# Graph attention and eight experts on one core: column tiles taken by twos, with more buffers for their weights

## Chip, core and metric

The kernel runs on one core of a Trainium2 chip. The metric is the device time in microseconds (us) of one launch. The kernel before takes 1325.94 us, the median of three runs (1325.19 to 1327.08). The profiled execution, from which the views below are taken, spans 1330.1 us from its first instruction to its last, at a mean granted TensorE clock of 0.991.

## What is computed

One layer: graph attention over 4096 nodes with 256 features and four heads, then a mixture of eight experts of which each node takes two. Cut to what matters here:

```python
h = einsum('nd,hdk->hnk', layernorm(x), W)           # 4 heads of 64
e = leaky_relu(s_row[:, :, None] + s_col[:, None, :], 0.2)
e = where(adj[None] > 0, e, NEG_INF)
att = softmax(e, axis=-1)
h_prime = einsum('hij,hjk->hik', att, h)
y = elu(h_prime) + x @ Wr + br                       # heads side by side
x = x + gamma * layernorm(y) + beta
x = x + moe(layernorm(x))                            # top 2 of 8, gelu(x @ W1) @ W2
```

The change is in the softmax's weights and in the two sums over them: the numerator (weights times h) and the denominator (weights summed).

## The kernel before

Output rows are taken in four stages of R = 1024 (the loop over a, line 1218); call them stage 0 to stage 3. Within a stage the loop over j (line 1220) takes 32 column tiles of 128 nodes. For each column tile:

- `load_mask` (line 1087) fetches 128 x 1024 numbers of the adjacency (three buffers) and ScalarE makes a bf16 mask of them (L1092 and L1093, three buffers).
- `weigh` (line 1199) makes the weights on VectorE: for each of the four heads one instruction (L1205) writes `w`, 128 x 1024 in fp32, as the larger of the row factor `er` and the column factor `eb`, times the mask. Each `w` lies in one of ten buffers of a pool, so a column tile takes four buffers, and ten buffers are two and a half tiles.
- `attend` (line 760) sums on TensorE. `sum_rows` (line 741) multiplies each head's weights, in two halves of 512 rows, with `ha`, a 128 x 64 block; two heads lie side by side in the columns of the array, and the results gather in four PSUM banks `acc`. `sum_weights` (line 750) multiplies the same weights with `unit`, two columns wide; four heads lie side by side, and the denominators gather in `den`. Each is eight matmuls per tile, and each of these is two records in the trace (fp32). Below, R stands for the rows of one column tile (16 records on L745) and W for its weights (16 records on L754).

A weights buffer is free again when both sums of its tile have read it. `queue` (line 407) chains the matmuls of both sums in the order in which they are written, so TensorE takes them in exactly that order. `attend` writes R before W for even tiles and for the last, and W before R for the others: R0 W0 W1 R1 R2 W2 W3 R3 and so on. TensorE thus changes between the two forms once per tile.

Other work lies between. In stage 0, blocks of 512 nodes are normed (`norm_block`, line 567), turned and projected (`project_block`, line 593) as the tiles need them; the first four tiles are done in halves of 512 rows. In stages 1 to 3 `finish_blocks` (line 917) carries the stage before to its end in steps, one per column tile: transposes on TensorE (L931, L960), elu, the norm (VectorE's L972, L975, L983, L989), the experts' choice (`route_rows`, line 780). These instructions are not in the chain of `queue`; a scheduler places them when the program is built. In stage 3 the plan of the first experts' tiles and the load of `w10`, the first expert's weights, are placed before the end (`first_tile`, line 1076). `mean_of_h` (line 714) needs all blocks and follows stage 0. After stage 3 come the experts: no weights of the attention are made there.

## Time and profile before

| | |
|---|---|
| median of 3 runs | 1325.94 us |
| span of the profiled execution | 1330.1 us |
| first rows of stage 0, 1, 2, 3 | 36.4, 282.3, 463.5, 644.5 us |
| end of the attention on TensorE | 826.7 us |
| TensorE, VectorE, ScalarE busy | 1287.9, 868.8, 574.1 us |

The page gives, for each engine, its busy time and its share of the span; then the span in 40 equal slices, each digit the busy share in tenths; then the costliest groups of instructions, each with line, engine, output<-inputs, shapes, count, busy time and the mean of one in ns, and after the second bar the idle time of the engine just before them and what ended it. A busy time of TensorE is a union of pipelined matmuls whose ends are modelled. The timeline merges neighbouring instructions of one kind: start, length, engine, line, names, shapes, count. The view of waits gives for each pair who waited for whom: total, number of times, longest.

### The profile page before, as it was taken

What the parts mean: (1) busy time and instruction counts of PE and PEld (TensorE: products, weight loads), DVE (VectorE), ACT (ScalarE), POOL (GpSimd) and SP (SyncE); (2) the same over time, 40 slices, a digit from 0 to 9 for tenths busy, and PEclk for the clock granted to TensorE, in tenths of its full rate; (3) what the DMA queues carried; (4) which work ended last, traced back from release to release, by engine and by line L of the source; (5) the groups of instructions that cost most, each with busy time, mean ns of one, the idle gap of its engine ahead of it and who ended that gap; (6) DMA issues with size and microseconds to landing.
All of it is one profiled execution on the core that took longest, in us unless ns stands there. A gap on an engine that the chain in (4) does not pass through costs nothing.

```text
span 1330.1 us, 19232 instructions
## 1 busy us (share of the span) xinstructions
PE 1287.9 (97%) x7019; PEld 679.3 (51%) x7019; DVE 868.8 (65%) x1746; ACT 574.1 (43%) x1016; POOL 232.5 (17%) x190
## 2 busy tenths in 40 slices
PE   6899999999999999999999999999999999999997
PEld 4423344322232222232222323888888877888886
DVE  4899887789999989999899996655111111121110
ACT  3423333346764457644576432533333332323332
POOL 1000000000005300015000150125222222122222
PEclk9899999999999999999999999999899999999999
DMA  5525243343443535534333342987756786888772
GB/s 164 204 84 174 96 111 96 112 158 100 131 136 109 194 98 140 138 107 153 96 111 111 106 133 60 350 249 213 245 155 188 189 183 146 197 203 209 175 208 53
DMA packets 144145, 202.42 MB, mean 152 GB/s; under 512 B 49728, under 2 KB 113872, under 8 KB 143392
## 3 DMA queue, kind: packets, MB, share of 16 engines
q1 hardware_dynamic: 122448, 161.26, 40.7%
q0 software_dynamic: 19360, 32.53, 10.9%
q10 hardware_dynamic: 2224, 7.22, 1.4%
q8 instruction: 59, 0.97, 0.3%
q14 instruction: 54, 0.44, 0.1%
HBM read 171.89 MB, written 29.08 MB: 151 GB/s over the span
## 4 chain that ended last, share of the span: by engine, by line
PE 57%; DMA 19%; DVE 17%; issue 5%; ACT 1%; another core or an unknown queue 0%; POOLq 0%; ACTq 0%; DVEq 0%
PE acc L745 24%; DMA out<-o,ids 18%; PE den L754 12%; DVE w L1205 12%; PE po L1384 8%; PE ph L1355 7%; PE pr L629 1%; PE ph L605 1%; DMA xb<-in_x 1%; DVE y L983 1%; DVE y L975 1%; PE pt L584 1%; DVE y L972 1%; PE pt L1337 1%; DVE y L989 0%
## 5 line engine op out<-in xcount | busy, mean ns | idle before, releaser
L1205 DVE SCALAR_TENSOR_TENSOR w<-er,eb,am 128x1024 f32<-128x1024 f32 x496 | 610.0, 1286 | 44.5 <-PE den L754 41.3
L745 PE MATMUL acc<-w,ha 128*64 128x512 f32 x2048 | 466.2, 599 | 5.3 <-DVE w L1205 4.6
L745 PEld LDWEIGHTS acc<-w,ha 128*64 128x64 f32 x2048 | 137.7, 137 | 301.6 <-issue 281.0
L1359 ACT ACTIVATE hT<-ph,bias 128x256 f32<-128x256 f32 (+1 forms) x264 | 126.3, 480 | 296.5 <-PE ph L1355 205.2
L1092 ACT ACTIVATE am<-adj 128x1024 bf16<-128x1024 int32 x124 | 131.1, 1057 | 283.8 <-DVE w L1205 275.2
L1355 PE MATMUL ph<-xT,w 128*128 128x256 f32 (+1 forms) x1056 | 242.3, 387 | 4.0 <-ACT hT L1359 2.5
L754 PE MATMUL den<-w,unit 128*2 128x512 f32 x2048 | 238.2, 592 | 5.5 <-DVE w L1205 5.5
L1384 PE MATMUL po<-w,hT 128*128 128x256 f32 x1088 | 241.9, 381 | 0.0
L1384 PEld LDWEIGHTS po<-w,hT 128*128 128x128 f32 x1088 | 206.7, 191 | 28.2
L1355 PEld LDWEIGHTS ph<-xT,w 128*128 128x128 f32 x1056 | 200.5, 190 | 39.4 <-ACT hT L1359 3.1
L1393 DVE SCALAR_TENSOR_TENSOR o<-po,share,b2s 128x256 f32<-128x256 f32 x67 | 32.3, 483 | 268.3 <-PE po L1384 246.8
L1396 POOL DMA_INDIRECT out<-o,ids x67 | 104.9, 1566 | 345.0 <-DMA out<-o,ids 215.6
L754 PEld LDWEIGHTS den<-w,unit 128*2 128x2 f32 x2048 | 43.5, 84 | 174.5 <-issue 151.8
L1093 ACT ACTIVATE am<-am 128x1024 bf16<-128x1024 bf16 x124 | 130.9, 1057 | 3.0
L909 POOL DMA_INDIRECT lists<-xe,at x64 | 92.0, 1437 | 134.3 <-DVE missed L888 39.5
L993 POOL DMA_DIRECT2D out<-y x6 | 4.7, 782 | 329.3 <-issue 155.6
L1341 DVE COPY xT<-pt 128x256 f32<-128x256 f32 x13 | 5.5, 423 | 66.3 <-PE pt L1337 66.3
L605 PE MATMUL ph<-wall,xT 128*128 128x264 f32 x112 | 30.6, 393 | 0.3 <-DVE sc L615 0.3
L1376 ACT ACTIVATE b2s<-b2b,share 128x256 f32<-128x256 f32 x68 | 30.8, 503 | 0.0
L629 PE MATMUL pr<-wr,xT 128*128 128x256 f32 x112 | 29.0, 384 | 0.2 <-ACT xT L588 0.2
L187 ACT ACTIVATE m<-y,off 128x256 f32<-128x256 f32 x48 | 23.8, 497 | 10.5 <-DVE off L184 10.5
L962 ACT ACTIVATE y<-ptr,z 128x64 f32<-128x64 f32 x96 | 22.0, 313 | 8.7 <-PE ptr L960 8.7
(316 smaller groups left out, 655.8 us busy)
## 6 DMA issues: line engine op xcount, KB each, us to landing
w<-in_L_ffn_W SPq DMA_DIRECT2D x66, 1024.0 KB
adj<-in_adj SPq DMA_DIRECT2D x128, 512.0 KB
er<-parts ACTq DMA_DIRECT2D x3, 2048.0 KB
b2b<-in_L_ffn_b SPq DMA_DIRECT2D x33, 128.0 KB
early<-lists SPq DMA_DIRECT2D x16, 260.0 KB
residual<-rb POOLq DMA_DIRECT2D x8, 512.0 KB
rb<-residual SPq DMA_DIRECT2D x8, 512.0 KB
out<-y POOLq DMA_DIRECT2D x8, 512.0 KB
```

The source lines that it names most:

```text
L605: nc.tensor.matmul(ph, xT[:, c, ts(t, P)], wall[:, c, :], start=(c == 0), stop=(c == DC - 1),)
L629: nc.tensor.matmul(pr[:, t % 2, :], xT[:, c, ts(t, P)], wr[:, c, :], start=(c == 0), stop=(c == DC - 1),)
L745: queue(nc.tensor.matmul(acc[half][h // 2][ts(h % 2, K), :], ha[:, j, ts(h, K)], w[half][h], start=(j == 0), stop=(j == NT - 1),))
L754: queue(nc.tensor.matmul(den[h * Q : h * Q + HB, :], unit[:, j, h, 1 - half : 1 - half + HB], w[half][h], start=(j == 0 and half == 0), st ...
L909: ins = nc.gpsimd.indirect_dma_start(lists, bass.IndirectOffsetOnAxis(ap=at[:, k, t : t + 1], axis=0), xe[:, t, :], None,).ins
L1092: nc.scalar.activation(am, at[:, 0], AF.Relu)
L1093: nc.scalar.activation(am, am, AF.Sign)
L1205: nc.vector.scalar_tensor_tensor(wh[:, these], er[:, these, h], eb[:, j, h : h + 1], mask[:, these], op0=OP.max, op1=OP.mult,)
L1355: order_of(nc.tensor.matmul(ph, job["w1"][:, c, ts(f, P)], xT[:, c, :], start=(c == 0), stop=(c == DC - 1),))
L1359: job["gelu"] = nc.scalar.activation(hT[:, f, :], ph, AF.Gelu, bias=job["bias"][:, f : f + 1]).ins
L1384: order_of(nc.tensor.matmul(po, hT[:, f, ts(k, CH)], w2[:, f, :], start=(f == 0), stop=(f == FC - 1)))
L1396: nc.gpsimd.indirect_dma_start(job["into"], bass.IndirectOffsetOnAxis(ap=ids[:, k : k + 1], axis=0), o, None, compute_op=OP.add,)
```

## The change

`attend` now takes column tiles by twos. For the first two of a group of four it writes R0 R1 W0 W1, for the next two W2 W3 R2 R3, so that TensorE changes the form once per two tiles; the last two tiles of a stage take rows first again. The first tiles of stage 0, done in halves, keep the old order. A tile's weights are thereby held longer, and `kept` keeps the first tile of a pair until its second sum.

For that, buffers are added from memory that lies idle: two halves of `w10` (which isn't loaded before stage 3), and, from the end of stage 0, the two turned blocks `turned[0]` and `turned[1]`, which only stage 0 reads. So there are 12 buffers in stage 0, 14 in stages 1 and 2, and 12 in stage 3, where `w10` is needed for its load. `made_w` counts the weights made and deals them out in turn: first the spare ones, then the ten of the pool. The lengthening of the file moves later lines by 13 (up to `weigh`) and up to 26.

```diff
+        kept = []
+
         def attend(w, j, halves):
-            rows_first = j % 2 == 0 or j == NT - 1
-            for add in (sum_rows, sum_weights) if rows_first else (sum_weights, sum_rows):
-                add(w, j, halves)
+            if len(halves) < HB:
+                for add in (sum_rows, sum_weights) if j % 2 == 0 else (sum_weights, sum_rows):
+                    add(w, j, halves)
+                return
+            both = (sum_rows, sum_weights)
+            if j // 2 % 2 and j < NT - 2:
+                both = (sum_weights, sum_rows)
+            both[0](w, j, halves)
+            if j % 2 == 0:
+                kept.append(w)
+            else:
+                both[1](kept.pop(), j - 1, halves)
+                both[1](w, j, halves)
...
                     for h in range(H):
-                        wh = work.tile([P, HB, B], F32, tag="w", name="w", bufs=10)
+                        nth = made_w[0] % (10 + len(spare))
+                        made_w[0] += 1
+                        if nth < len(spare):
+                            wh = spare[nth]
+                        else:
+                            wh = work.tile([P, HB, B], F32, tag="w", name="w", bufs=10)
...
+                made_w = [0]
+                spare = [w10[:, c].rearrange("p (s r) -> p s r", s=HB) for c in range(DC)]
...
                     er = later
+                    if a == 0:
+                        spare += [turned[b].rearrange("p (s c) r -> p s (c r)", s=HB) for b in (0, 1)]
+                    if a + 2 == NR:
+                        del spare[:DC]
```

## The prediction

> **What bounds the kernel now.** I read the page first: busy shares, slices, costliest groups.

> ```profile
> PE 1287.9 (97%) x7019; PEld 679.3 (51%) x7019; DVE 868.8 (65%) x1746; ACT 574.1 (43%) x1016; POOL 232.5 (17%) x190
> PE   6899999999999999999999999999999999999997
> DVE  4899887789999989999899996655111111121110
> L1205 DVE SCALAR_TENSOR_TENSOR w<-er,eb,am 128x1024 f32<-128x1024 f32 x496 | 610.0, 1286 | 44.5 <-PE den L754 41.3
> L745 PE MATMUL acc<-w,ha 128*64 128x512 f32 x2048 | 466.2, 599 | 5.3 <-DVE w L1205 4.6
> L754 PE MATMUL den<-w,unit 128*2 128x512 f32 x2048 | 238.2, 592 | 5.5 <-DVE w L1205 5.5
> ```

> TensorE is full everywhere; VectorE is nearly full until the attention ends, at 826.7 us, and then nearly idle. So the change, all in the attention, works where two engines are both close to the limit. The windows of stages 1 to 3 (a = 1, 2, 3) put a number on that:

> ```profile
> 282.00:463.00 181.00, 178.78 (x1115) 50.52 (x1115) 171.65 (x231) 102.64 (x163) 34.45 (x20) 1.00 0.44 132
> 463.00:644.00 181.00, 179.09 (x1109) 50.52 (x1103) 170.93 (x227) 104.36 (x164) 26.76 (x20) 1.00 0.43 123
> 644.00:826.00 182.00, 178.92 (x1107) 51.50 (x1103) 168.22 (x251) 92.29 (x152) 25.17 (x18) 1.00 0.33 103
> ```

> Columns are width, then busy PE, PEld, DVE. VectorE has 9 to 14 us to spare in 181. The waits of stage 3 say who waits:

> ```profile
> DVE w L1205 <- PE den L754: 4.8, 5, 2.7
> PE den L754 <- DVE w L1205: 1.4, 2, 0.9
> ```

> VectorE waits for buffers more than TensorE for weights. Now the pitch, from TensorE's timeline in a quiet stretch of stage 2 (start, length, count):

> ```profile
> 598.59 7.09 PE L745 MATMUL acc<-w,ha 128*64 128x512 f32 x32
> 605.60 3.62 PE L754 MATMUL den<-w,unit 128*2 128x512 f32 x32
> 609.15 7.09 PE L745 MATMUL acc<-w,ha 128*64 128x512 f32 x32
> 616.17 3.62 PE L754 MATMUL den<-w,unit 128*2 128x512 f32 x32
> ```

> Two column tiles take 609.15 - 598.59 = 10.56 us. A block of 16 rows matmuls alone lasts 3.65, one of 32 7.09, so one tile's rows (R) cost 3.44; likewise weights (W) 3.62 - 1.90 = 1.72. Two of each are 10.32; the remaining 0.24 is two switches between R and W, 0.12 each. And VectorE beside it:

> ```profile
> 607.52 9.68 DVE L1205 SCALAR_TENSOR_TENSOR w<-er,eb,am 128x1024 f32<-128x1024 f32 x8 [0.88 <-PE den L754]
> 618.08 6.08 DVE L1205 SCALAR_TENSOR_TENSOR w<-er,eb,am 128x1024 f32<-128x1024 f32 x5 [0.88 <-PE den L754]
> ```

> Eight w in 9.68 with the last lasting 1.28: pitch 1.20, a tile 4.8 us. VectorE stands 0.88 us, then starts 607.52 - 605.60 = 1.92 us after the W that frees its buffer began. I use that: a buffer last read by a W is filled again from 1.92 us after that W's start.

> [...] 0.12 us at each change between the 64-column and the 32-column form, nothing between W and W. [...] The VectorE records of before stand in program order.

> **The change part by part.** *Switches.* In the order in which the two programs put the matmuls, changes of form (R, W, other) per stage go 75 to 75, 65 to 43, 62 to 45, 58 to 39. In stage 0 norms and projections fall between more blocks, so nothing is won. Stages 1 to 3 lose 22, 17 and 19, at 0.12: 2.6, 2.0 and 2.3 us, 7.0 in sum, on TensorE and so on the path, if weights are there in time.

> *The wait it adds.* Take four tiles in the new order, R0 from 0: R0 R1 to 6.88, W0 from 7.0, W1 8.72, W2 10.44, W3 due 12.16, R2 from 14.0, R3 to 20.88. That is 20.88 for 21.12 before. Each tile takes four buffers, and a W needs all four. With 12 buffers (stages 0 and 3) tile 3 reuses tile 0's, read last by W0: VectorE may start at 7.0 + 1.92 = 8.92 and ends at 8.92 + 3 x 1.20 + 1.28 = 13.8, when W3 was due at 12.16. TensorE stands 1.64 us in every four tiles: 22.52 for 21.12, 1.4 worse. Queued behind W3 are R2 and R3, nothing else can pass. With 14 buffers (stages 1, 2) only the last two w of tile 3 wait: 8.92 + 1.20 + 1.28 = 11.4, in time by 0.76. In the order before, w were 2.6 to 3.1 us ahead of their first matmul in quiet stretches (start of a tile's first matmul less end of its fourth w).

> *Stage 0.* Tiles 4 to 7: the w of these run without a gap from 80.7 to 99.9, so W7 can't start before 99.95, and R6 and R7 stand behind it: 99.95 + 1.72 + 0.12 + 6.88 = 108.7, where R7 ended at 106.4; +2.3. From 8 to 27 the stall is 1.64 less what stands between W2 and W3: three transposes (0.65) in three groups, a projection (0.5), the means (1.0): 3 x 1.0 + 1.1 + 0.6 = +4.7. TensorE waited 2.5 us for xn there; those transposes come later now, I take back two thirds, -1.7. The means of h, alone between the stages before (with the wait for u behind, 1.6 us), move into a stall: -1.6. Sum +3.7, between 0 and +7.

> *Stages 1, 2.* The finishing of the last stage puts about 6.9 us per block on VectorE (1.15 for L972, 1.38 for four L975, 1.62 for four L983, 1.63 for four L989, small ones), most just ahead of the last w of a group of four. In stage 2, tile 7: its third w waits for W4's buffer, then L983 comes, then the fourth: TensorE waits about 1.0; in stage 1 about 1.6. Before, such waits (den and acc for w) summed to 1.5 in each stage, so they cancel, and the switches stay as gain: -2.2 each, between 0 and -4.

> *Stage 3.* Up to tile 15 VectorE is the bound in tiles 4 to 11 both ways (before: no gap from 671.4 to 731.8). Tile 11 is ready about when it was (64.5 against 65.6 us into the stage), but W11, R10, R11 then follow instead of W11, R11: +2.3, of which 1.3 comes back by tile 16, because over 30 other matmuls stand inside W12 to W15 and cover the stall. Groups 16, 20, 24: 3 x (1.64 - 0.24) = +4.2. The last group runs R R W W twice, with two tiles each, and needs no fourth W in a row: -0.3. Sum +4.9, between +2 and +7.

> *Held at nothing:* moved mask and row loads (three tiles of masks are held ahead as before), w10 as a buffer (free until its load in stage 3, still well ahead of the experts), the experts after 826.7 (same order; they move with the attention's end).

> Total: 3.7 - 2.2 - 2.2 + 4.9 = +4.2 us, 1330.1.

> **Rivals.** *Switches win* (0.25): VectorE keeps so far ahead that none of the stalls counted above (4.7 in stage 0 and 3 x 1.64 in stage 3, 9.6 together) is there: 1330.1 - 9.6 = 1320.5. For: VectorE waits for buffers, not the reverse, and gets more of them. Against: 12 buffers are three tiles, and W3 comes 5.16 us after W0's start, while refilling needs 1.92 + 4.88. *A draw* (0.24): stage 0 gives back more (all xn waits, a better order of projections, +0.5 instead of +3.7): 1326.9. *VectorE becomes the bound* (0.16): the bursts cost another 2 us in each of stages 1 and 2, and the xn waits stay: 1330.1 + 4 + 1.7 = 1335.8. For: zero slack in tiles 7 to 17 before. Against: 9 us spare per stage. My forecast has 0.35.

> **Numbers.** Likeliest 1330.1. Ends of the terms: 0 - 4 - 4 + 2 = -6 and 7 + 0 + 0 + 7 = +14, both improbable in sum; the range takes in the first rival and the last with a little beyond each: 1319 to 1337. The first rival is under 1323.3 (faster, 0.25), the draw within 0.2% (0.24), the other two over 1328.6 (slower, 0.51).

> **What would show it.** R and W blocks of 32 in stages 1 to 3, four tiles in 20.9 us in quiet stretches of stages 1 and 2 but 22.5 in stage 3, with den waiting about 1.6 us for w before the fourth W there. VectorE waiting for den in all stages. Stages 1 and 2 some 179 us long, stage 3 some 187. It is wrong if stage 3 keeps 21 us per four tiles, or if the bursts make acc or den wait over 3 us in stage 1.

## The result, and the profile after

The kernel after takes 1337.99 us (1335.52 to 1340.48) beside 1325.57 us of the kernel before, four runs of each: a ratio of 1.0093, 95% interval 1.0069 to 1.0116. It is slower by about 12.4 us where 4.2 were forecast, and 1 us outside the range. The page of the kernel after, busy shares and groups:

```profile
PE 1280.3 (96%) x7019; PEld 682.9 (51%) x7019; DVE 868.7 (65%) x1746; ACT 572.1 (43%) x1016; POOL 226.7 (17%) x190
L1223 DVE SCALAR_TENSOR_TENSOR w<-er,eb,am 128x1024 f32<-128x1024 f32 x440 | 540.4, 1276 | 50.4 <-PE den L754 35.3
L745 PE MATMUL acc<-w,ha 128*64 128x512 f32 x1824 | 416.3, 598 | 7.9 <-DVE w L1223 7.9
L754 PE MATMUL den<-w,unit 128*2 128x512 f32 x1824 | 237.5, 598 | 21.2 <-DVE w L1223 21.2
```

TensorE's waits for weights have grown: den stood 21.2 us for `w` where it stood 5.5, acc 7.9 where it stood 5.3. Of acc's waits, 4.9 and 3.1 us lie ahead of the very first R of stage 0, before any length below is counted. (The groups hold fewer `w` than before, 440 and not 496, because those made in the turned blocks are listed apart as `xT`: 56.) Where, the stages show. Lengths from the first R of a stage to the first R of the next, and for stage 3 to the end of the attention, read from the starts of the matmuls on L745 and L754:

| us | stage 0 | stage 1 | stage 2 | stage 3 |
|---|---|---|---|---|
| before | 245.9 | 181.1 | 181.1 | 182.1 |
| after | 248.4 | 183.7 | 178.4 | 191.1 |
| difference | +2.5 | +2.6 | -2.7 | +9.0 |
| forecast | +3.7 | -2.2 | -2.2 | +4.9 |

The differences sum to 11.4. The spans of the two profiled executions differ by 8.7 only, and are not to be compared as they stand: the experts took 503.5 us in that of before and 497.3 to 500.2 in all others, and the first R came between 34.9 and 39.7 us into the span, from run to run, in all kernels here. Stage lengths leave both out.

In their quiet stretches stages 2 and 3 differ in one thing, 14 buffers or 12. TensorE's timeline of the kernel after in a quiet stretch of stage 2 (start, length, count):

```profile
615.26 5.75 PE L754 MATMUL den<-w,unit 128*2 128x512 f32 x50
622.24 3.65 PE L745 MATMUL acc<-w,ha 128*64 128x512 f32 x16
```

Four W start at 615.26, and the next R at 622.24: 6.98 us, which is 4 x 1.72 and a switch of 0.10. Nothing stands. The same in stage 3, then VectorE beside it:

```profile
788.96 0.60 PE L754 MATMUL den<-w,unit 128*2 128x512 f32 x2 [1.58 <-DVE w L1223]
811.57 1.02 PE L754 MATMUL den<-w,unit 128*2 128x512 f32 x5 [1.57 <-DVE w L1223]
```

```profile
784.03 1.28 DVE L1223 SCALAR_TENSOR_TENSOR w<-er,eb,am 128x1024 f32<-128x1024 f32 x1 [0.27 <-PE den L754]
785.23 2.47 DVE L1223 SCALAR_TENSOR_TENSOR xT<-er,eb,am 128x1024 f32<-128x1024 f32 x2
787.62 10.93 DVE L1223 SCALAR_TENSOR_TENSOR w<-er,eb,am 128x1024 f32<-128x1024 f32 x9
```

W20 starts at 782.04. VectorE starts the four `w` of tile 23 at 784.03, 1.99 us later (two of the four lie in turned blocks, `xT`), and the fourth ends at 787.62 + 1.28 = 788.90; W23 starts at 788.96, after 1.58 us of standing, and the next one of its kind after 1.57. From 788.96 to 811.57 are 22.6 us per four tiles. That is the timetable of the prediction, with 22.52 and 1.64. The windows of stages 1 to 3 of the kernel after (width, then busy PE, PEld, DVE):

```profile
288.00:471.00 183.00, 177.25 (x1119) 53.09 (x1119) 177.21 (x236) 104.72 (x164) 27.20 (x20) 1.00 0.45 134
471.00:650.00 179.00, 176.76 (x1113) 52.49 (x1103) 171.15 (x228) 103.25 (x163) 31.47 (x20) 1.00 0.45 127
650.00:841.00 191.00, 179.98 (x1107) 52.90 (x1103) 168.08 (x249) 91.22 (x149) 21.50 (x18) 0.98 0.31 96
```

TensorE is busy 1.5 and 2.3 us less in stages 1 and 2 than before (178.78 and 179.09): the switches are saved, of which 2.6 and 2.0 were forecast. The column behind the five engines is the granted clock. In stage 3 TensorE is idle for 11 us of 191 and its clock is 0.98 in the mean, while VectorE has 23 us to spare. So no engine is the bound of that stage as a whole: they wait for each other, though VectorE is full in parts of it. And the waits of stage 3 (who waited for whom: total, times, longest), then of stage 1:

```profile
PE den L754 <- DVE w L1223: 9.5, 5, 2.7
```

```profile
PE den L754 <- DVE w L1223: 2.9, 3, 1.6
PE den L754 <- DVE xT L1223: 0.4, 1, 0.4
```

Before, den waited 1.4 us for `w` in stage 3; now 9.5. In stage 1 it is 2.9, and 3.3 with the weights that lie in turned blocks. The forecast holds for stages 0 and 2 and for the quiet part of stage 3; what was to be found out is why stage 1 lost and why stage 3 lost twice what was worked out. Times of four-tile steps, from the start of one group of four to that of the next, tell where:

| us | tiles 0-3 | 4-7 | 8-11 | 12-15 | 16-19 | 20-23 | 24-27 | 28-31 |
|---|---|---|---|---|---|---|---|---|
| stage 1 before | 22.5 | 22.9 | 23.2 | 22.4 | 24.9 | 22.9 | 21.1 | 21.3 |
| stage 1 after | 25.2 | 22.8 | 21.7 | 23.7 | 24.4 | 23.5 | 21.4 | 21.1 |
| stage 2 before | 23.2 | 22.9 | 23.2 | 22.4 | 24.9 | 22.1 | 21.1 | 21.3 |
| stage 2 after | 22.9 | 21.4 | 23.5 | 22.9 | 24.5 | 21.3 | 20.9 | 21.1 |
| stage 3 before | 24.0 | 23.2 | 23.7 | 25.7 | 22.0 | 21.1 | 21.1 | 21.2 |
| stage 3 after | 23.9 | 26.3 | 26.5 | 24.5 | 23.8 | 22.6 | 22.6 | 21.0 |

Stage 1 loses in its first group, stage 3 in tiles 4 to 11 (+5.9), and in the three quiet groups (+4.8, forecast +4.2).

### The profile page after: what moved, and what is told of

Read it like the earlier page. It is cut to its first block, busy times and chain, and to the rows that moved or that the text cites. A ratio compares the mean times of both kernels' runs of the same rounds, so it can differ in the third digit from the quotient of the medians.

```text
span 1338.8 us, 19200 instructions
## 1 busy us (share of the span) xinstructions
PE 1280.3 (96%) x7019; PEld 682.9 (51%) x7019; DVE 868.7 (65%) x1746; ACT 572.1 (43%) x1016; POOL 226.7 (17%) x190
## 5 line engine op out<-in xcount | busy, mean ns | idle before, releaser
L1223 DVE SCALAR_TENSOR_TENSOR w<-er,eb,am 128x1024 f32<-128x1024 f32 x440 | 540.4, 1276 | 50.4 <-PE den L754 35.3
L745 PE MATMUL acc<-w,ha 128*64 128x512 f32 x1824 | 416.3, 598 | 7.9 <-DVE w L1223 7.9
L745 PEld LDWEIGHTS acc<-w,ha 128*64 128x64 f32 x1824 | 125.5, 137 | 270.1 <-issue 244.6
L754 PE MATMUL den<-w,unit 128*2 128x512 f32 x1824 | 237.5, 598 | 21.2 <-DVE w L1223 21.2
L1410 PEld LDWEIGHTS po<-w,hT 128*128 128x128 f32 x1088 | 205.5, 190 | 27.7
L754 PEld LDWEIGHTS den<-w,unit 128*2 128x2 f32 x1824 | 44.6, 84 | 169.4 <-issue 134.1
L922 POOL DMA_INDIRECT lists<-xe,at x64 | 85.8, 1341 | 127.4 <-DVE missed L901 39.5
L1223 DVE SCALAR_TENSOR_TENSOR xT<-er,eb,am 128x1024 f32<-128x1024 f32 x56 | 70.0, 1277 | 3.1 <-PE acc L745 1.4
L745 PE MATMUL acc<-xT,ha 128*64 128x512 f32 x224 | 57.9, 595 | 0.0
L754 PE MATMUL den<-xT,unit 128*2 128x512 f32 x224 | 55.7, 607 | 0.4 <-DVE xT L1223 0.4
L745 PEld LDWEIGHTS acc<-xT,ha 128*64 128x64 f32 x224 | 15.5, 137 | 33.1 <-issue 31.6
```

The lines of the kernel that those rows point to most:

```text
L745: queue(nc.tensor.matmul(acc[half][h // 2][ts(h % 2, K), :], ha[:, j, ts(h, K)], w[half][h], start=(j == 0), stop=(j == NT - 1),))
L754: queue(nc.tensor.matmul(den[h * Q : h * Q + HB, :], unit[:, j, h, 1 - half : 1 - half + HB], w[half][h], start=(j == 0 and half == 0), st ...
L922: ins = nc.gpsimd.indirect_dma_start(lists, bass.IndirectOffsetOnAxis(ap=at[:, k, t : t + 1], axis=0), xe[:, t, :], None,).ins
L1223: nc.vector.scalar_tensor_tensor(wh[:, these], er[:, these, h], eb[:, j, h : h + 1], mask[:, these], op0=OP.max, op1=OP.mult,)
L1410: order_of(nc.tensor.matmul(po, hT[:, f, ts(k, CH)], w2[:, f, :], start=(f == 0), stop=(f == FC - 1)))
```

## Experiments

Times are medians, each with its ratio to the kernel before in the same series; diffs are against the kernel after unless said otherwise. Four-tile steps and stage lengths are read as above, from one profiled execution of each version. They repeat well: stage 1 is 183.7 us long in each of the three profiles that have the kernel after's order and turn of buffers there, and 180.6 or 180.7 in each of the four with the other turn that is tried below.

### Order without buffers, buffers without order, and both

**Sixteen buffers in stage 3.** `er0`, the row factors of stages 0 and 2, is idle in stage 3 and gives four.

```diff
-                        del spare[:DC]
+                        flat = er0.rearrange("p s h r -> p (s h r)").rearrange("p (k i) -> p k i", k=H)
+                        spare[:] = spare[DC:] + [flat[:, k].rearrange("p (s r) -> p s r", s=HB) for k in range(H)]
```

> The changed kernel, with 16 buffers for weights instead of 12 in stage 3 (four pieces of er0, which stage 3 doesn't read). Theory A, the 12 buffers are what stage 3 loses by (three tiles' worth, so the fourth W of a group stands until the first W has been read, and twice the array then runs at half clock): stage 3 (191.1 us in the changed kernel, 182.2 before) falls to about 180, with four tiles in 20.9 us where it is quiet and no half-clock stretch; total about 11 us less than the changed kernel, some 1327. Theory B, VectorE's bursts from finishing the stage before are the bound in tiles 4 to 15: only the three quiet groups gain, 4 to 5 us; stage 3 stays near 186, total about 1333.

Measured: 1331.45 us, ratio 1.0037 (1.0020 to 1.0053). Stage 3 is 183.4 us, quiet groups 20.9, tiles 4 to 7 and 8 to 11 at 22.2 and 23.1 where the kernel after takes 26.3 and 26.5. The waits of TensorE in stage 3 of this run:

```profile
PE den L754 <- DVE w L1223: 0.2, 1, 0.2
```

TensorE is busy as long as in the kernel after (179.7 of 183 in the window of stage 3, against 180.0 of 191); the 9.5 us of den's waits are 0.2. So four more buffers take back most of the loss of stage 3, in its full part as well as in the quiet one. That is theory A's cause, but not its size: stage 3 was to take about 180 us without a stretch at half clock, and the total to be some 1327. Much of what is missing lies where stage 2 hands over to stage 3. Stage 2 is 181.8 us long in this run, 3.4 more than in the kernel after, all of it in its last group (24.4 for 21.1), at whose end TensorE stands for a weight in a turned block:

```profile
648.86 1.08 PE L745 MATMUL acc<-xT,ha 128*64 128x512 f32 x4 [3.27 <-DVE xT L1223]
```

By the clock's own records TensorE then runs at half clock from 650.1 to 653.5 (the mean from 649 to 832 is 0.98), and stage 3's first group takes 25.5 us, not 23.9. The count of weights made is 400 there, and 400 modulo 16 is 0: next in turn are the turned blocks, which hold weights of stage 2's tile 30 and are read last by its W30. The next section finds the same at the end of stage 0; in the ring of the last version stage 2 and stage 3's first group are back at 179.5 and 23.9 us.

**The buffers alone**, old order:

```diff
-            if len(halves) < HB:
...
-                both[1](w, j, halves)
+            rows_first = j % 2 == 0 or j == NT - 1
+            for add in (sum_rows, sum_weights) if rows_first else (sum_weights, sum_rows):
+                add(w, j, halves)
```

> The order of before (R W, W R) with the changed kernel's 12, 14, 12 buffers. Theory A, the loss is the order's, not the buffers': stages as before within 1 us each, total 1324 to 1327. Theory B, buffers on other memory (w10, the turned blocks) or the change of their number at a stage's end cost by themselves: 3 us or more above before, most of it where stage 1 begins. Theory C, more buffers help the old order, whose small waits of TensorE for weights (about 1.5 us per stage) go: total 1320 to 1322.

Measured: 1327.77 us, ratio 1.0008 (0.9997 to 1.0019); stages 246.9, 181.2, 181.2, 182.3, all within 1 us of before. Buffers that the order has no use for bring nothing here, and dealing them out by hand costs nothing that these runs can tell.

**By twos in stages 1 and 2 alone**, buffers as in the kernel after; where `by_twos[0]` is false, `attend` takes the order of before (that part of the edit is not shown):

```diff
+                    by_twos[0] = a in (1, 2)
```

> Twos only in stages 1 and 2 (14 buffers); stages 0 and 3 in the order of before with 12. Theory A, 12 buffers are what twos lose by: stage 0 as before (246), stage 2 about 178.4, stage 3 about 182, stage 1 179 to 181; total 3 to 5 us below before, 1321 to 1323. Theory B, twos cost by themselves (VectorE bound): stages 1 and 2 no shorter than before, total 1326 or more.

Measured: 1323.52 us, ratio 0.9979 (0.9970 to 0.9988). Stages 246.7, 179.9, 178.4, 182.4. Stage 1 gains 1.2 us here though it lost 2.6 in the kernel after: with the same order and buffers inside the stage, this points to how stage 0 hands over to it.

### The handing over from stage 0

At the end of stage 0 two buffers are added, and the turn in which buffers are dealt out goes from modulo 12 to modulo 14, with the count running on. The count is then 144, and 144 modulo 14 is 4: next in turn are the pool's buffers, tile 29's two and then tile 30's four, while the halves of `w10` (used by tile 29) and the turned blocks, free for long, are dealt at 0 to 3 and have just been passed over. In the new order tile 30's weights are read last by W30, which comes after R31 (244.9 us into stage 0; before, W30 came right after R30, at 236.5). W30 starts at 284.54. The timeline of the kernel after on VectorE:

```profile
275.94 7.26 DVE L1223 SCALAR_TENSOR_TENSOR w<-er,eb,am 128x1024 f32<-128x1024 f32 x6 [3.22 <-issue]
286.45 12.05 DVE L1223 SCALAR_TENSOR_TENSOR w<-er,eb,am 128x1024 f32<-128x1024 f32 x10 [3.25 <-PE den L754]
```

VectorE makes six `w`, four of tile 31 and two of stage 1's tile 0, then stands 3.25 us for W30 (286.45 is 1.91 after 284.54), with free buffers beside it (the next two that lie in turned blocks are made from 298.42): the `w` that waits holds up those behind it. The run that tests it deals the added ones first:

```diff
-                        spare += [turned[b].rearrange("p (s c) r -> p s (c r)", s=HB) for b in (0, 1)]
+                        spare[:0] = [turned[b].rearrange("p (s c) r -> p s (c r)", s=HB) for b in (0, 1)]
+                        made_w[0] = 0
...
-                        del spare[:DC]
+                        del spare[DC:]
```

> The changed kernel, but at the end of stage 0 the turn of the buffers starts anew with the two turned blocks, then the two halves of w10. In the changed kernel tile 0 of stage 1 stood 3.25 us for buffers of tile 30 while four others were free. Theory A, that standing is what stage 1 loses by: stage 1 falls from 183.7 to about 181, total 2 to 3 us below the changed kernel. Theory B, the loss at the start of stage 1 is the wait of stage 0's last tiles for 12 buffers and only moves: stage 1 stays within 1 us of 183.7.

Measured: 1336.28 us, ratio 1.0072 (1.0052 to 1.0093). Stages 248.4, 180.6, 179.5, 191.0. Stage 1 is 3.1 us shorter, stage 2 1.1 longer (its first group takes 23.5 and its seventh 21.4, for 22.9 and 20.9; why was not followed). VectorE of this run at the same place:

```profile
270.35 2.47 DVE L1223 SCALAR_TENSOR_TENSOR xT<-er,eb,am 128x1024 f32<-128x1024 f32 x2
273.60 9.65 DVE L1223 SCALAR_TENSOR_TENSOR w<-er,eb,am 128x1024 f32<-128x1024 f32 x8 [0.78 <-PE den L754]
284.16 2.48 DVE L1223 SCALAR_TENSOR_TENSOR w<-er,eb,am 128x1024 f32<-128x1024 f32 x2 [0.91 <-PE den L754]
```

Ten weights where there were six, two of them in turned blocks (`xT`), are made before the same W30 (this run lies 2.3 us earlier in its span); VectorE stands 0.91 us for it and not 3.25. Shown: the loss of stage 1 against before was the turn of the buffers, not VectorE's bursts. The lengths of the stage show it; the totals gain 1.7 us, and their intervals overlap. Den's waits in stage 1 go from 3.3 to 1.9 us.

### The clock in stage 3

In tiles 4 to 11 of stage 3 the windows of the kernel after show something else (width, busy PE, PEld, DVE, ACT, POOL, then the granted clock):

```profile
686.00:689.00 3.00, 0.97 (x8) 0.42 (x4) 3.00 (x6) 1.90 (x9) 0.00 (x0) 1.00 0.59 173
689.00:692.00 3.00, 2.92 (x14) 0.50 (x18) 3.00 (x12) 1.61 (x4) 0.00 (x0) 0.55 0.32 67
713.00:716.00 3.00, 0.73 (x7) 0.50 (x5) 3.00 (x6) 2.97 (x5) 0.00 (x0) 1.00 0.26 100
716.00:720.00 4.00, 3.55 (x18) 0.59 (x20) 4.00 (x7) 2.49 (x3) 0.00 (x0) 0.58 0.34 97
```

TensorE does almost nothing in 686 to 689 and 713 to 716, in which it waits for the weights of W7 and W11 (2.11 and 2.72 us); in the stretches behind it the clock is 0.55 and 0.58, for 3.4 us each by the clock's own records, and the W there take 0.85 us per four records and not 0.43. Does that make stage 3's excess? By theory A idle matmuls, put into the standing, keep the clock up; they compute nothing that is used:

```diff
+                        if a + 1 == NR and j in (7, 11):
+                            fill = bank([P, B], "fill")
+                            n = 9 if j == 7 else 12
+                            for i in range(n):
+                                queue(nc.tensor.matmul(
+                                    fill, all1, all1[:, :1].to_broadcast([P, B]),
+                                    start=(i == 0), stop=(i == n - 1),
+                                ))
```

> The changed kernel, with 9 and 12 idle matmuls on ones (result unused) put in TensorE's order just before W7 and W11 of stage 3, where it stood 2.4 and 3.0 us and then ran 3.4 us at half clock; they fit into the standing. Theory A, the standing itself lowers the clock: no half-clock stretch near tiles 7 and 11, the four-matmul steps of W11 come at 0.43 us and not 0.85, stage 3 falls from 191.1 to about 187.7. Theory B, the slow matmuls come from something else (VectorE reaching the same memory, waits inside the W): the steps stay at 0.85 and stage 3 at 191, or longer by what the idle matmuls take.

Measured: 1339.24 us, ratio 1.0093 (1.0074 to 1.0112), the time of the kernel after. TensorE's timeline of this run, at W11 and W15:

```profile
709.14 2.78 PE L1263 MATMUL fill<-all 128*128 128x512 bf16 x11
713.31 0.60 PE L754 MATMUL den<-w,unit 128*2 128x512 f32 x2 [1.27 <-DVE w L1223]
713.74 0.60 PE L754 MATMUL den<-w,unit 128*2 128x512 f32 x2
737.14 1.90 PE L754 MATMUL den<-w,unit 128*2 128x512 f32 x16 [1.72 <-DVE w L1223]
```

With 2.78 us of idle matmuls in the gap the W behind it start 0.43 us apart and not 0.85: theory A is right in that the standing lowered the clock. Stage 3 is 191.6 us all the same. W11 came 1.2 us earlier into the stage (65.0 against 66.2) and ran in half the time, but at W15 TensorE now stood 1.72 us for weights in one piece, and tiles 12 to 15 take 26.7 us, not 24.5. What the clock took in the kernel after it took from time in which TensorE would have waited for VectorE anyway. The half clock is there, and by this run it costs nothing at the end of the stage: theory A's 187.7 us were missed.

### How few buffers cost what

```diff
-                spare = [w10[:, c].rearrange("p (s r) -> p s r", s=HB) for c in range(DC)]
+                spare = []
...
-                    if a == 0:
-                        spare += [turned[b].rearrange("p (s c) r -> p s (c r)", s=HB) for b in (0, 1)]
-                    if a + 2 == NR:
-                        del spare[:DC]
```

> The changed kernel's order with the ten buffers of before in all stages. The last w of a group of four then wait for W1 and the six from the tenth on for W0 and W1: by my timetable W3 comes 4.0 us late, so four quiet tiles take 20.88 + 4.0 = 24.9 us (22.5 with 12 buffers, 20.9 with 14). Theory A, timetable and clock: 24.9, and where the standing lowers the clock 1.7 more, up to 26.6; stages 1 and 2 some 25 to 40 us longer. Theory B, VectorE's own pace is the limit and not the buffers: stages 1 and 2 change by under 5 us against the changed kernel.

Measured: 1425.01 us in one run, so without an interval. A quiet group of stage 3 takes 24.9 us:

```profile
868.15 1.90 PE L754 MATMUL den<-w,unit 128*2 128x512 f32 x16 [2.89 <-DVE w L1223]
893.10 2.34 PE L754 MATMUL den<-w,unit 128*2 128x512 f32 x12 [2.89 <-DVE w L1223]
```

893.10 - 868.15 = 24.95. By the prediction's timetable, ten buffers make six `w` wait for W0: 8.92 + 5 x 1.20 + 1.28 = 16.2 for a W3 due at 12.16, so 20.88 + 4.04 = 24.92. Quiet groups at 10, 12, 14 and 16 buffers are thus 24.9, 22.6, 20.9 and 20.9: below 14 each two buffers that are missing cost about 2 us per four tiles; more than 14 bring nothing there. The whole stages are longer than that (205.5, 210.9 and 215.4 for 1 to 3; stages 1 and 2 by 21.8 and 32.5 us over the kernel after, where 25 to 40 were expected), since the full parts lose too and the clock fell to half in more places (its mean over the span is 0.978, beside 0.991 before). The line at 893.10 has one: 12 records in 2.34 us (the view ends there), and that group of four takes 26.6, 1.7 more.

### A version that takes what was learned

The order by twos in stages 1 to 3 only; buffers in a ring, in which those that become free are dealt first and the turn of all others is kept; `er0`'s four in stage 3. `ring` begins as `lent`, the two halves of `w10`, and ten times None, which stands for a buffer of the pool:

```diff
+                    by_twos[0] = a > 0
...
-                        nth = made_w[0] % (10 + len(spare))
-                        made_w[0] += 1
+                        wh = ring.pop(0)
+                        ring.append(wh)
...
+                        ring[:0] = [turned[b].rearrange("p (s c) r -> p s (c r)", s=HB) for b in (0, 1)]
...
+                        ring[:] = [r for r in ring if not any(r is t for t in lent)]
+                        ring[:0] = [flat[:, k].rearrange("p (s r) -> p s r", s=HB) for k in range(H)]
```

> Meant to beat both: twos in stages 1, 2 and 3, stage 0 in the order of before; buffers 12, 14, 14 and 16 (w10's two halves give way to four pieces of er0 in stage 3), kept as a ring in which a free buffer comes next when the number changes. Theory A, the order gains wherever no W waits for a buffer: stages 0 to 3 of about 246.5, 179, 178.5 and 179 to 180, no half-clock stretch between first rows and experts; total 1319 to 1321 against 1323.5 with twos in stages 1 and 2 alone. Theory B, stage 3's bursts eat the gain there: stage 3 at 182 or more, total 1323 or more.

Measured: 1322.39 us (1321.69 to 1326.32), ratio 0.9969 (0.9956 to 0.9983): faster than both kernels, though less than hoped. It is not shown to be faster than twos in stages 1 and 2 alone (ratio 0.9979): the intervals overlap, and its stages sum to 688.0 us where that run's sum to 687.4. Stages 246.1, 180.7, 179.5, 181.7. Stage 3 loses nothing now, but it gains nothing either: its steps are 23.9, 22.2, 23.0, 28.0, 21.9, 20.9, 20.9, 21.0. What tiles 4 to 11 win, tiles 12 to 15 give back (28.0 for 25.7). There a transpose waits for ScalarE:

```profile
735.60 0.33 PE L808 MATMUL ptx<-ident,xe 128*128 128x128 f32 x1 [1.15 <-ACT xe L792]
```

And just behind it lies a stretch at half clock, which theory A had excluded (windows; the granted clock is the 1.00 and the 0.50):

```profile
733.67:737.08 3.41, 1.94 (x11) 0.71 (x7) 3.41 (x4) 2.88 (x5) 0.00 (x0) 1.00 0.51 154
737.09:740.49 3.40, 3.40 (x32) 1.55 (x30) 3.40 (x4) 2.29 (x4) 0.00 (x0) 0.50 0.00 0
```

The run below that keeps the old order up to tile 15, with sixteen buffers too, has such a stretch in tiles 12 to 15 as well (732.4 to 735.8); the kernel before, with ten, has none there, its granted clock being 1.00 from 644 to 826. 3.4 us at half clock are at most 1.7 us of matmul time (an estimate from these lines), of the 2.3 that these tiles lose, and here no wait for weights follows that would have hidden it: den's waits for weights are 0.2 us in the whole stage. No run takes this stretch away, so its share is not shown.

Two more runs ask about the two stages that are left. Both are against this version.

**By twos in stage 0 too**, `by_twos[0] = True`:

> The ring of buffers of ring_twos_1_3 (sixteen buffers in stage 3), but column tiles by twos in stage 0 too. Theory A, each stage's cost is its own: stage 0 is 248.5 us long (before 245.9, ring_twos_1_3 246.1), tiles 8 to 11 take near 27.8 us instead of 23, and stages 1 to 3 stay at 180.7, 179.5 and 181.7 us, so the time is 2 to 3 us over ring_twos_1_3 and near that of the kernel before (1324 to 1326). Theory B, the loss of stage 0 is given back in stage 1, because VectorE uses TensorE's standing to get ahead: stage 1 is 2 us shorter and the time that of ring_twos_1_3 within 0.5 us.

Measured: 1326.34 us, ratio 0.9994 (0.9986 to 1.0003). Stages 249.0, 180.7, 179.5, 181.6: stage 0 costs 2.9 us, and nothing of it comes back later. The waits of stage 0, of the kernel before and after, say how:

```profile
PE acc L745 <- DVE w L1205: 4.3, 3, 3.1
PE pt L584 <- DVE xn L579: 3.1, 4, 0.9
PE den L754 <- DVE w L1205: 1.5, 3, 0.7
```

```profile
PE acc L745 <- DVE w L1223: 7.2, 4, 4.9
PE pt L584 <- DVE xn L579: 0.6, 1, 0.6
PE den L754 <- DVE w L1223: 7.2, 8, 1.6
```

Den's waits grow by 5.7 us, and those of the transposes for `xn` fall by 2.5. Acc's lines hold the waits ahead of the very first R (3.1 and 4.9 us); within the stage they grow by 1.1.

**By twos in stage 3 only from tile 16**:

```diff
+                        by_twos[0] = 0 < a < NR - 1 or (a == NR - 1 and j >= 16)
```

> The ring of buffers of ring_twos_1_3, but in stage 3 column tiles by twos only from tile 16 on; tiles 0 to 15 keep the old order. Theory A, the order itself costs where VectorE is the bound, since R before W needs the weights of two tiles before either W: tiles 12 to 15 of stage 3 take 25.7 to 26.7 us again instead of 28.0, groups from 16 on stay at 20.9, stage 3 is 180 to 181 us long instead of 181.7 and the time 0.5 to 1.5 us under ring_twos_1_3. Theory B, the loss of tiles 12 to 15 is VectorE's own backlog and comes in any order: tiles 4 to 15 take the same 73.2 us in sum as in ring_twos_1_3, and the time is the same or up to 0.5 us more.

Measured: 1323.76 us, ratio 0.9967 (0.9952 to 0.9982). Stage 3 is 182.5 us, tiles 12 to 15 take 28.3 us in the old order too, and tiles 0 to 15 98.5 us against 97.1. Theory B is nearer: tiles 4 to 15 take 74.0 us, not less than the 73.2, and the loss in tiles 12 to 15 comes with either order. In the old order these tiles take 25.7 us with ten buffers, 26.7 with twelve and 28.3 with sixteen. That it is a backlog of VectorE is not shown: TensorE waits there for ScalarE, and then runs at half clock (732.4 to 735.8 in this run). The new order is worth 1.4 us of stage 3 in tiles 0 to 15, given buffers, of which tiles 16 to 19 give back 0.6; the times of the two versions don't tell them apart.

## Why the prediction was wrong in size

**The timetable of four tiles was right.** 20.88 forecast with 14 buffers, 20.9 measured; 22.52 with 12, 22.6 measured; W3 late by 1.64, 1.58 measured. W7 of stage 0 was to start at 99.95 us and R7 to end at 108.7 with the first R at 36.4; it started 63.66 after the first R, so at 100.1, and R7 began 68.97 after it, so it ended at 36.4 + 68.97 + 3.44 = 108.8.

**Stage 2** was forecast at -2.2 and came at -2.7, **stage 0** at +3.7 and +2.5 (+2.9 in the run that isolates it), inside its bounds. In stage 0 TensorE's idle time grows from 7.0 to 10.5 us, by 3.5, about what was counted; its busy time falls by 1.0 (238.9 to 237.9), where the forecast had nothing to win.

**Stage 1 failed, by 4.8 us (-2.2 forecast, +2.6 measured), at a step that wasn't there.** The list of what is held at nothing weighs `w10`'s memory and the mask loads, but not the turn in which buffers are dealt. "Each tile takes four buffers, and a W needs all four" was applied with the oldest buffer always the next in turn. This is true inside a stage; where the number of buffers changes, the code deals by a count modulo that number and the oldest isn't next. Resetting the turn took 3.1 us back. The remaining 1.7 are a part of the gain that didn't come: with the turn reset stage 1 wins 1.5 us in tiles 4 to 7 and loses 1.0 in sum elsewhere; why was not followed. Den waiting over 3 us in stage 1 was named as what would refute the forecast. It waited 3.3 (2.9 for `w`, 0.4 for `xT`), and 1.9 with the turn reset: the sign appeared, but by the turn, since the bursts alone stay below it.

**Stage 3 failed in the size of one term: tiles 4 to 15.** The step reads: tile 11 ready 64.5 us into the stage, W11, R10, R11 behind it, so R12 later by 2.3, and 1.3 of it back by tile 16. Measured, R12 comes 5.7 later (76.6 against 70.9) and R16 4.5 later. W11 starts at 66.2, 1.7 after the forecast, and takes 3.4 us and not 1.7 because of the clock: 66.2 + 3.4 + 6.9 = 76.5. The 1.3 did come back (5.7 - 4.5 = 1.2). VectorE stood 1.40 us for ScalarE ahead of its L985 in tile 11, a wait that the kernel before doesn't have:

```profile
704.89 1.22 DVE L985 SCALAR_TENSOR_TENSOR y<-y,m 128x1024 f32<-128x1024 f32 x1 [1.40 <-ACT m L983]
```

But the clock isn't the cause of the time, as its run showed, and the order alone is not either (the row by twos with sixteen buffers is from the ring; with the turn left as it was, stage 3 took 183.4 and stage 2 3.4 more):

| stage 3 | 12 buffers | 16 buffers |
|---|---|---|
| old order | 182.3 | 182.5 (old order to tile 15) |
| by twos | 191.1 | 181.7 |

Twelve buffers serve the old order, and the new one costs nothing with sixteen; both together cost 9. The prediction treated tiles 4 to 11 as bound by VectorE in both orders, and put the shortage of buffers into the quiet groups alone. The runs show that the shortage costs there too, 4.0 of the 4.5 us (tiles 0 to 15 take 101.1 us with 12 and 97.1 with 16). Two runs give the cleanest pair: the one with the turn reset and the one by twos in all stages take the same order and the same buffers up to the end of stage 2 (their stages 0 to 2 agree within 0.6 us) and differ in stage 3's buffers alone, 12 against 16. Stage 3 takes 191.0 and 181.6 us, tiles 0 to 15 101.0 and 97.0.

The timelines of the same two runs show by what path. With twelve buffers VectorE stands over 3 us ahead of tile 3's weights; in the kernel after it does so until 1.98 us after W0 began at 657.25 (the view names no engine for this wait):

```profile
659.23 3.68 DVE L1223 SCALAR_TENSOR_TENSOR w<-er,eb,am 128x1024 f32<-128x1024 f32 x3 [3.29 <-issue]
```

With sixteen it needs no buffer of tile 0 there. When the full part begins, 23.4 us into the stage in both, with the first instruction of L985 (L990 in the ring's file), VectorE has made 27 weights and not 23. The second instruction of that line, with which the finishing of the second block of 512 begins, comes behind 50 weights and not 42, so behind tile 11's weights (44 to 47, counted from 0) and not ahead of them. Tile 11 is complete at 55.4 us with sixteen buffers and at 66.2 with twelve (65.5 in the kernel before). The order of VectorE's instructions, which the scheduler sets, is thus not the same in the two programs; how much of the 4.0 us is the wait and how much that order, no run separates.

**The rivals.** "Switches win" describes what happens when buffers suffice, but only in stages 1 and 2 (1323.52 and not 1320.5). "VectorE becomes the bound", the forecast nearest to the time, was near for other reasons: of its two terms, the waits for `xn` did not stay (3.1 us before, 0.6 after), and stage 2 gained more than forecast; VectorE had 6, 8 and 23 us to spare in stages 1, 2 and 3. The range was too narrow at its upper end since each stage's bound came from the one timetable, which cannot show what happens at a handing over.

## What to carry to other kernels

When a new order holds buffers longer, count how late the last consumer's buffer is refilled (here 1.92 us after the reading block starts, and 1.2 us for each of its instructions); if the sum is more than the order's lead, the loss recurs in every group. Where the producing engine is full it can be larger for a while (here 3.8 us a group in tiles 4 to 11 against 1.7 in the quiet ones, most of which tiles 12 to 15 gave back). If buffers are added or withdrawn in the middle, follow which one is dealt next just there: a count modulo a new number can pick the one that is busiest while others lie free. A change that is a loss in sum may be a gain in some stages: lengths stage by stage, not the total, say which part to keep.

## What the runs showed of the hardware that was not expected

In the kernel after, TensorE stood 2.11 us ahead of W7 and 2.72 us ahead of W11 of stage 3, and a stretch of 3.41 us at half clock came behind each: by the clock's records from 689.32 and from 716.63. That is at most 1.7 us of matmul time each (an estimate, half of 3.41). A length alone does not decide it: in the ten-buffer run the two lines shown follow gaps of 2.89 us each, and the first W runs at full clock (16 records in 1.90 us), the second not (12 records in 2.34 us).

```profile
862.84:866.25 3.41, 1.90 (x16) 0.31 (x16) 3.41 (x4) 2.12 (x2) 0.00 (x0) 1.00 0.25 55
866.26:869.66 3.40, 1.51 (x16) 0.32 (x16) 3.40 (x4) 1.50 (x2) 0.00 (x0) 1.00 0.25 94
890.15:893.55 3.40, 0.51 (x12) 0.12 (x11) 3.40 (x4) 0.76 (x2) 0.00 (x0) 1.00 0.00 0
893.56:896.97 3.41, 3.41 (x18) 0.57 (x12) 1.88 (x2) 1.63 (x2) 0.00 (x0) 0.50 0.01 2
```

TensorE is busy 1.90 and 1.51 us in the two steps that share the first gap, and full clock follows both; it is busy 0.51 us in the step that holds the second, and the next step is at half clock. The two gaps are equally long and differ in where they lie on the grid. No limit of the busy time is shown: full clock followed 1.51 us here, and half clock followed 1.94 us in the version by twos in stages 1 to 3 (733.67 to 737.08, shown above).
